# The end of a two-layer graph kernel: the last round's empty slots filled, and the last group's softmax weights transposed on TensorE without the detour through DRAM

**Chip, cores, metric.** One core of one Trainium2 chip. The metric is the device time of the core in microseconds (us), median of several runs.

## The reference, cut to what matters

128 graphs of 128 nodes with 512 features pass two layers, each with residual and layer norm:

```python
# layer 0
q, k, v = x @ Wq0.T, x @ Wk0.T, x @ Wv0.T
rel = adj.T * (q @ k.T);  rel = rel / norm(rel, axis=2)
x = layernorm(x + rel @ v)
# layer 1: 8 heads of 64
q, k, v = (x @ W + b for W, b in ((Wq,bq), (Wk,bk), (Wv,bv)))
scores = q @ k.T / 8 + where(adj == 0, -1e9, 0)
x = layernorm(x + softmax(scores) @ v)
```

All is fp32.

## The kernel before

It works on 32 groups of 4 graphs. TensorE's work is cut into slots, 35 to a round. In round r five projections run, 7 slots each: m and v0 (layer 0) of group r+1, then q, k and v1 (layer 1) of group r. All else is hung on slots as short pieces; a piece named at slot s is issued to its engines just before that slot's projection step.

The schedule of layer 1's attention, for graph b of group g:

```python
for b in range(G):
    s = 32 + 7 * b
    at(g, s, attn_scores, g, b)
    at(g, s + 1, attn_max, g, b)
    for i in range(4):
        at(g, s + 2 + i, attn_exp, g, b, 2 * i)
    at(g, s + 4, attn_spill, g, b, 0)
    at(g, s + 6, attn_spill, g, b, 1)
    at(g, s + 7, attn_stage, g, b)
    at(g, s + 12, attn_transpose, g, b)
    at(g, s + 13, attn_out, g, b)
    at(g, s + 14, attn_back, g, b)
    at(g, s + 16, attn_rows, g, b)
    at(g, s + 18, attn_sum, g, b)
    at(g, s + 20, attn_stats, g, b)
    at(g, s + 22, attn_store, g, b)
```

The kernel transposes these weights on VectorE in blocks of 32x32 (the prediction below names the page that bears on it), so the blocks of the 128x128 weights are sorted through DRAM: `attn_spill` writes them (wd), `attn_stage` reads them back in another order (wl), `attn_transpose` gives wT. The value product comes out transposed and makes a second detour (od, then the row tile o):

```python
def attn_out(g, b):
    ...
            nc.tensor.matmul(p[s*HD:(s+1)*HD, a, :], V1[g][:, b, h*HD:(h+1)*HD], wT[...])   # po
    nc.vector.transpose(oT..., p...)
    ...
def attn_rows(g, b):
    o = two.tile(..., tag="o")
    nc.sync.dma_start(o..., OD.pop((g, b))...)
    xr = two.tile([P, D], F32, tag="xr")
    nc.sync.dma_start(xr, X1D[g, b // 2][b % 2])       # residual
def attn_sum(g, b):
    nc.vector.tensor_tensor(f, f, rs..., op=ALU.mult)  # "the row product", o<-o,rs
    nc.gpsimd.tensor_tensor(xr, xr, bv_b, op=ALU.add)
    nc.gpsimd.tensor_tensor(o, o, xr..., op=ALU.add)
```

Layer 0's result also goes through DRAM, for the block order that layer 1 needs:

```python
def x1_spill(g, h):      # x1d<-x
    X1D[g, h] = dram.tile([2, P, D], F32, tag="x1d", bufs=6)
    nc.sync.dma_start(X1D[g, h]..., X[g, h])
def x1_stage(g, h):      # xl_h<-x1d, four transfers; they must wait until x1d has landed
    load_staged(g, h, X1D[g, h])
```

All these transfers are issued by one engine, SyncE, in program order.

Of the kernel before, what the change touches and what calls it, by code (L numbers as in the profile page):

```python
# [6 lines left out]

F32 = mybir.dt.float32
AF = mybir.ActivationFunctionType
ALU = mybir.AluOpType  # L10
AX = mybir.AxisListType

EPS = 1e-5
NEG = -1e9
# [3 lines left out]
def kernel(  # L18
# [15 lines left out]
    nc = tc.nc  # L34
    B, N, D = x.shape
    P = 128
    H, HD = 8, 64
    G = 4
    NG = B // G
    C = D // P  # L40
    HF = D // 2
    assert N == P and D == H * HD and B % G == 0 and G * N == D

    const = ctx.enter_context(tc.tile_pool(name="const", bufs=1))
    one = ctx.enter_context(tc.tile_pool(name="one", bufs=1))
    two = ctx.enter_context(tc.tile_pool(name="two", bufs=2))
# [64 lines left out]
    bv_b = const.tile([P, D], F32, name="bv_b")  # L111
    nc.sync.dma_start(bv_b, bass.AP(tensor=bv1.tensor, offset=bv1.offset, ap=[[0, P], [1, D]]))

    ones = const.tile([P, 1], F32, name="ones")
    nc.vector.memset(ones, 1.0)
    mhalf = const.tile([P, G], F32, name="mhalf")
    nc.vector.memset(mhalf, -0.5)

    mask = const.tile([P, D], F32, name="mask")
    for a in range(H // 2):  # L120
        nc.vector.tensor_scalar(mask.rearrange("p (q a r) -> p q a r", q=A, a=H // 2)[:, :, a, :],
# [94 lines left out]

    def x1_transpose(g, dh, h):
        if dh == 0 and h == 0:
            X1T[g] = one.tile([P, C, G, P], F32, tag="x1T", name=f"x1T_{g}")
            TX1[g] = one.tile([P, 4, 2, HF], F32, tag="tx1", name=f"tx1_{g}")  # L220
        transpose_quarter(X1T[g], g, h, dh)
        if h:
            token_sums(TX1[g], X1T[g], dh)
# [4 lines left out]
    class Projection:  # L228
# [8 lines left out]
        def begin(self):  # L237
            k, g = self.kind, self.g
            if k in ("m", "v0"):
                self.xT, self.t = XT[g], TX[g]  # L240
            else:
                self.xT, self.t = X1T[g], TX1[g]
            if k == "m":
                YT[g] = self.y = one.tile([P, C, G, P], F32, tag="yT", name=f"yT_{g}")
            elif k == "q":
                QT[g] = self.y = one.tile([P, C, G, P], F32, tag="qT", name=f"qT_{g}")
            elif k == "k":
                KT[g] = self.y = one.tile([P, C, G, P], F32, tag="kT", name=f"kT_{g}")
            elif k == "v0":
                V0[g] = self.y = one.tile([P, G, D], F32, tag="v0", name=f"v0_{g}")  # L250
            else:
                V1[g] = self.y = one.tile([P, G, D], F32, tag="v1", name=f"v1_{g}")
            self.s = one.tile([P, 3, 2, HF], F32, tag="s", name=f"s_{self.name}")

        def out(self, eh, th):
# [81 lines left out]
    def statistics(h, stats, b, tag):  # L337
        bs = small.tile([P, 6], F32, tag="bs", name=f"bs_{tag}")
        nc.vector.bn_stats(bs, h)  # L339
        nc.vector.bn_aggr(stats[:, b, :], bs)  # L340

    def inverse_std(stats, n, tag):
        ve = small.tile([P, G], F32, tag="ve", name=f"ve_{tag}")
        nc.gpsimd.tensor_scalar(ve[:, :n], stats[:, :n, 1], EPS, None, op0=ALU.add)
        rstd = small.tile([P, G], F32, tag="rstd", name=f"rstd_{tag}")
        nc.gpsimd.tensor_tensor(rstd[:, :n], ve[:, :n], mhalf[:, :n], op=ALU.pow)
        return rstd
# [28 lines left out]
    def attn_scores(g, b):  # L376

        p = ps_s.tile([P, 2, A, H // 2, Q], F32, tag="s", name=f"ps_{g}_{b}")
        for a in range(H // 2):
            for s in range(2):  # L380
                r = slice(s * HD, (s + 1) * HD)
                nc.tensor.matmul(p[:, s, :, a, :], QT[g][r, a, b, :], KT[g][r, a, b, :], start=True, stop=True)  # L382
        w = two.tile([P, 2, A, H // 2, Q], F32, tag="w", name=f"w_{g}_{b}")
        nc.vector.scalar_tensor_tensor(w.rearrange("p s q a r -> p s (q a r)"),  # L384
                                       p.rearrange("p s q a r -> p s (q a r)"), HD ** -0.5,
                                       mask[:, None, :].to_broadcast([P, 2, D]), op0=ALU.mult, op1=ALU.add)
        nmax = small.tile([P, H], F32, tag="nmax", name=f"nmax_{g}_{b}")
        sums = small.tile([P, H], F32, tag="sums", name=f"sums_{g}_{b}")
        SOFT[g, b] = [w, nmax, sums]
# [19 lines left out]

    def attn_stage(g, b):  # L410

        wl = one.tile([P, A, H, Q], F32, tag="wl", name=f"wl_{g}_{b}")
        SOFT[g, b][0] = wl
        rows = WD.pop((g, b)).rearrange("(a s) q t f -> s a q (t f)", s=Q)
        for q in range(A):
            nc.sync.dma_start(wl[q * Q:(q + 1) * Q].rearrange("p a i r -> p a (i r)"), rows[:, :, q, :])
# [61 lines left out]




    R = 35
    dense, short = {}, {}

    def at(r, k, f, *a):
        short.setdefault(R * r + k, []).append((f, a))

    for r in range(-1, NG):
        todo = [("m", r + 1), ("v0", r + 1), ("q", r), ("k", r), ("v1", r)]
        for j, (kind, g) in enumerate(todo):  # L490
            if not 0 <= g < NG:
                continue
            pr = Projection(kind, g)
            for k, i in ((0, 1), (1, 5), (3, 6), (4, 2), (5, 3), (6, 7), (9, 4)):
                dense[R * r + 7 * j + k] = (pr, i)
    halves = [(dh, h) for dh in range(2) for h in range(2)]
    for g in range(NG):

        for h in range(2):
            if g:  # L500
                at(g - 2, 12, load_staged, g, h)
                at(g - 1, 12 + 4 * h, load, g, h)
            at(g - 1, 29 + h, x1_spill, g, h)
            at(g - 1, 30 + 2 * h, x1_stage, g, h)
        for k, (dh, h) in zip((24, 25, 27, 28), halves):
            at(g - 2, k, x_transpose, g, dh, h)
        for b in range(G):
            at(g - 1, 11 + b, l0_score, g, b)
            at(g - 1, 19 + 2 * b, l0_out, g, b)
            at(g - 1, 27 + b // 2, l0_layernorm, g, b)  # L510
        at(g - 1, 16, l0_norm, g)
        at(g - 1, 26, l0_rstd, g)

        for k, (dh, h) in zip((1, 2, 4, 5) if g else (8, 9, 11, 12), halves):
            at(g, k, x1_transpose, g, dh, h)
        for b in range(G):
            s = 32 + 7 * b
            at(g, s, attn_scores, g, b)
            at(g, s + 1, attn_max, g, b)
            for i in range(4):  # L520
                at(g, s + 2 + i, attn_exp, g, b, 2 * i)
            at(g, s + 4, attn_spill, g, b, 0)
            at(g, s + 6, attn_spill, g, b, 1)
            at(g, s + 7, attn_stage, g, b)
            at(g, s + 12, attn_transpose, g, b)
            at(g, s + 13, attn_out, g, b)
            at(g, s + 14, attn_back, g, b)
            at(g, s + 16, attn_rows, g, b)
            at(g, s + 18, attn_sum, g, b)
            at(g, s + 20, attn_stats, g, b)  # L530
            at(g, s + 22, attn_store, g, b)

    with tc.manual_schedule():
        for k in range(min(short), -R):
# [41 lines left out]
```

## Time and profile before

| | before |
|---|---|
| median of 4 runs | 2,628.34 us (2,625.99 to 2,632.44) |
| span of the profiled run | 2,625.2 us |
| start of the last projection step ahead of the value product of group 29's last graph ("the anchor") | 2,484.21 us |
| from the anchor to the end ("the end part") | 141.0 us |

The prediction below shows the views that carry its reading. The anchor is added here because it is the same instruction in every kernel of this document and no change reaches its own work. One more view shows the start: after the first loads (9.88 us), this is TensorE's only long wait in the first 60 us (start, duration, engine, operation, then the idle time before it and what ended it).

```profile
43.63 3.78 PE L268 MATMUL pb_v<-wc_v,tx 128*128 128x256 f32 x8 [4.56 <-DVE yT L283]
```

VectorE is late there with yT, since masks and sums of weights stand ahead of it in its queue.

### The profile page before, as it was taken

Reading aid. Unit: us, or ns where it says so; the run is one execution under the profiler, and the core shown is the slowest. Engines: PE = TensorE matmul, PEld = TensorE weight load, DVE = VectorE, ACT = ScalarE, POOL = GpSimd, SP = SyncE. Lnnn points to the kernel's source line nnn. Section 1 sums busy time; section 2 is a strip of 40 time slices with the busy share of each in tenths; the row PEclk is TensorE's granted clock in tenths of the full one; section 3 lists DMA queues with packets and bytes.
Section 4 is the critical chain, followed back from the end, with each engine's and each line's share of the span. In section 5 each row is a group of like instructions: output and inputs, shape, how many; then the busy total and the mean of one; then the engine's idle time right before and its main releaser. Section 6 shows DMA issues by size and latency. Waiting matters only on the chain.

```text
span 2625.2 us, 41633 instructions
## 1 busy us (share of the span) xinstructions
PE 2540.0 (97%) x14624; PEld 2123.9 (81%) x14624; DVE 1607.3 (61%) x2584; ACT 1042.1 (40%) x3207; POOL 858.4 (33%) x1209
## 2 busy tenths in 40 slices
PE   7999999999999999999999999999999999999982
PEld 5788888888888888888888888888888888888861
DVE  4555665656666665666666666666666666666553
ACT  1234444444444434444344344344443434444442
POOL 4123332333332323333323333323333323333222
PEclk9999999999999999999999999999999999999985
DMA  6255556555555555555555545556545556546444
GB/s 149 68 142 167 152 167 168 155 159 165 159 159 173 158 153 168 159 155 173 164 148 176 159 149 173 161 151 176 161 146 174 161 157 174 161 142 176 152 140 130
DMA packets 518450, 412.09 MB, mean 157 GB/s; under 512 B 38240, under 2 KB 433632, under 8 KB 518240
## 3 DMA queue, kind: packets, MB, share of 16 engines
q1 hardware_dynamic: 518240, 409.43, 53.8%
q8 instruction: 115, 1.88, 0.3%
q14 instruction: 95, 0.78, 0.1%
HBM read 241.50 MB, written 167.77 MB: 156 GB/s over the span
## 4 chain that ended last, share of the span: by engine, by line
PE 93%; DMA 2%; DVE 2%; SPq 1%; POOL 1%; issue 1%; ACT 0%; DVEq 0%; POOLq 0%; ACTq 0%
PE pa_v L268 17%; PE pa_k L268 9%; PE pa_q L268 8%; PE pb_v L268 8%; PE pa_m L268 8%; PE ps L382 5%; PE po L433 5%; PE pst L320 4%; PE pd_v L268 4%; PE pb_k L268 4%; PE po L364 4%; PE pb_q L268 4%; PE pb_m L268 4%; PE pd_q L268 2%; PE pd_m L268 2%; PE pd_k L268 2%
## 5 line engine op out<-in xcount | busy, mean ns | idle before, releaser
L401 ACT ACTIVATE w<-w,nmax 128x128 f32<-128x128 f32 x1024 | 399.3, 393 | 330.4 <-DVE nmax L394 290.6
L461 POOL TENSOR_TENSOR xr<-xr,bv_b 128x512 f32<-128x512 f32 x128 | 164.1, 1282 | 694.8 <-DMA xr<-x1d 686.2
L268 PE MATMUL pa_v<-wc_v,tx 128*128 128x256 f32 x1536 | 372.2, 385 | 1.6 <-DVE v L283 1.6
L268 PEld LDWEIGHTS pa_v<-wc_v,tx 128*128 128x128 f32 x1536 | 281.7, 190 | 45.9 <-ACT kT L279 5.3
L459 DVE TENSOR_TENSOR o<-o,rs 128x512 f32<-128x512 f32 x128 | 121.8, 952 | 196.7 <-DMA o<-od 196.7
L384 DVE SCALAR_TENSOR_TENSOR w<-ps,mask 128x1024 f32<-128x1024 f32 x128 | 156.1, 1220 | 138.4 <-PE ps L382 137.8
L322 POOL TENSOR_TENSOR sq<-rel 128x128 f32<-128x128 f32 x128 | 51.6, 403 | 474.5 <-DVE rel L321 474.5
L401 ACT ACTIVATION_READ_ACCUMULATOR w<-w,nmax 128x1 f32 x1024 | 194.5, 190 | 0.0
L433 PE MATMUL po<-wT,v 128*64 128x128 f32 x2048 | 145.1, 286 | 47.5 <-DVE wT L420 46.5
L462 POOL TENSOR_TENSOR o<-o,xr 128x512 f32<-128x512 f32 x128 | 175.2, 1369 | 38.8 <-DVE o L459 27.8
L433 PEld LDWEIGHTS po<-wT,v 128*64 128x64 f32 x2048 | 113.3, 140 | 89.8 <-DVE wT L420 46.0
L268 PE MATMUL pa_q<-tx,wc_q 128*128 128x256 f32 x768 | 185.6, 385 | 0.0
L339 DVE BATCH_NORM_STATS2 bs<-o 128x6 f32<-128x512 f32 x128 | 87.8, 686 | 159.3 <-POOL o L462 159.3
L268 PE MATMUL pa_k<-tx,wc_k 128*128 128x256 f32 x768 | 184.7, 383 | 0.0
L268 PE MATMUL pa_m<-tx,wc_m 128*128 128x256 f32 x768 | 182.6, 381 | 0.3 <-ACT s_m L276 0.3
L436 DVE STREAM_TRANSPOSE oT<-po 128x512 f32<-128x512 f32 x128 | 91.8, 717 | 136.1 <-PE po L433 136.0
L268 PEld LDWEIGHTS pa_q<-tx,wc_q 128*128 128x128 f32 x768 | 144.1, 191 | 37.2 <-issue 14.6
L276 ACT COPY s_v<-pa_v 128x512 f32<-128x512 f32 x128 | 75.0, 586 | 231.6 <-PE pa_v L268 206.8
L268 PEld LDWEIGHTS pa_m<-tx,wc_m 128*128 128x128 f32 x768 | 146.8, 191 | 21.2 <-ACT s_m L276 1.0
L475 ACT ACTIVATE y<-o,sh,rstd 128x512 f32<-128x512 f32 x128 | 104.0, 813 | 149.1 <-POOL sh L354 142.5
L268 PEld LDWEIGHTS pa_k<-tx,wc_k 128*128 128x128 f32 x768 | 143.4, 190 | 23.6 <-issue 5.3
L394 DVE TENSOR_REDUCE nmax<-w 128x4 f32<-128x512 f32 x256 | 162.3, 676 | 0.1
(138 smaller groups left out, 5008.4 us busy)
## 6 DMA issues: line engine op xcount, KB each, us to landing
wd<-w SPq DMA_DIRECT2D x256, 256.0 KB, 2.5
wl<-wd SPq DMA_DIRECT2D x512, 128.0 KB, 2.8
xl_x<-in_x_dram SPq DMA_DIRECT2D x256, 128.0 KB, 5.5
x<-in_x_dram SPq DMA_DIRECT2D x64, 512.0 KB, 5.2
x1d<-x SPq DMA_DIRECT2D x64, 512.0 KB, 3.2
xl_h<-x1d SPq DMA_DIRECT2D x256, 128.0 KB, 2.6
od<-oT SPq DMA_DIRECT2D x512, 64.0 KB, 1.7
o<-od SPq DMA_DIRECT2D x128, 256.0 KB, 4.1
```

Source lines behind the costliest of these rows:

```text
L268: nc.tensor.matmul(bank[:, m, :], l[:, k, m * P:(m + 1) * P], r[:, k, :], start=start and m == 0 and k == 0, stop=(m == 1 and k == 1), ski ...
L320: nc.tensor.matmul(p, XT[g][:, dc, b, :], YT[g][:, dc, b, :], start=(dc == 0), stop=(dc == C - 1))
L364: nc.tensor.matmul(p, REL[g][0][:, b, :], V0[g][:, b, :], start=True, stop=True)
L382: nc.tensor.matmul(p[:, s, :, a, :], QT[g][r, a, b, :], KT[g][r, a, b, :], start=True, stop=True)
L384: nc.vector.scalar_tensor_tensor(w.rearrange("p s q a r -> p s (q a r)"), p.rearrange("p s q a r -> p s (q a r)"), HD ** -0.5, mask[:, Non ...
L394: nc.vector.tensor_reduce(nmax[:, s * (H // 2):(s + 1) * (H // 2)], w[:, s].rearrange("p q a r -> p a q r"), axis=AX.XY, op=ALU.max, negat ...
L401: nc.scalar.activation(w[:, s, :, a, :], w[:, s, :, a, :], AF.Exp, bias=nmax[:, i:i + 1], accum_out=sums[:, i:i + 1])
L433: nc.tensor.matmul(p[s * HD:(s + 1) * HD, a, :], V1[g][:, b, h * HD:(h + 1) * HD], wT[:, s * (H // 2) + a].rearrange("p q t -> p (q t)"), ...
L459: nc.vector.tensor_tensor(f, f, rs.rearrange("p s y a -> p (s y a)")[:, :, None].to_broadcast([P, A * H // 2, Q]), op=ALU.mult)
L461: nc.gpsimd.tensor_tensor(xr, xr, bv_b, op=ALU.add)
L462: nc.gpsimd.tensor_tensor(o, o, xr.rearrange("p (a f r) -> p f a r", a=H // 2, f=A), op=ALU.add)
L475: nc.scalar.activation(y.rearrange("p (a f r) -> p f a r", a=H // 2, f=A), o, AF.Identity, bias=sh[:, 0:1], scale=rstd[:, 0:1])
```

## The change

Intent: (1) In the last round there is no group 32, so m and v0 leave 14 empty slots; q, k and v1 of the last group move up into them, its layer 0 finishes a few slots earlier, and the attention of group 30 follows in 3 slots a graph, not 7. (2) The last group's weights stay on the chip: scores in plain head order, transposes on TensorE against an identity, a value product that comes out in rows, no wd, wl, od, o.

Cut to its core (lines with tags of buffers left out):

```diff
+    ident = const.tile([P, P], F32, name="ident")
+    make_identity(nc, ident)
+    maskp = const.tile([P, N], F32, name="maskp")
+    nc.vector.tensor_scalar(maskp, adj_sb, 0.0, NEG, op0=ALU.is_equal, op1=ALU.mult)
...
+    def last_residual(g):
+        LT["x"] = one.tile([P, G, D], F32, tag="qT", name=f"xr_{g}")
+        for h in range(2):
+            xr = LT["x"][:, 2 * h:2 * h + 2, :]
+            nc.sync.dma_start(xr, X1D[g, h].rearrange("b n d -> n b d"))
+            nc.gpsimd.tensor_tensor(xr, xr, bv_b[:, None, :].to_broadcast([P, 2, D]), op=ALU.add)
...
+    def last_transpose(g, b, s):
...
+        p = ps_m.tile([P, H // 2, P], F32, tag="m", name=f"pwT_{g}_{b}_{s}")
+        for a in range(H // 2):
+            nc.tensor.transpose(p[:, a, :], SOFT[g, b][0][:, s * (H // 2) + a, :], ident)
+        nc.vector.tensor_copy(LT[b // 2][:, b % 2, s * (H // 2):(s + 1) * (H // 2), :], p)
+
+    def last_out(g, b):
...
+        p = ps_b.tile([P, H, HD], F32, tag="d", name=f"po1_{g}_{b}")
+        for h in range(H):
+            nc.tensor.matmul(p[:, h, :], LT[b // 2][:, b % 2, h % 2 * (H // 2) + h // 2, :],
+                             V1[g][:, b, h * HD:(h + 1) * HD], start=True, stop=True)
...
+        nc.vector.tensor_tensor(o..., p, rs..., op=ALU.mult)
+        nc.vector.tensor_tensor(o, o, xr, op=ALU.add)
+        ... statistics, last_store: scale and store
...
-        todo = [("m", r + 1), ("v0", r + 1), ("q", r), ("k", r), ("v1", r)]
+        todo = [("m", r + 1), ("v0", r + 1)] if r < NG - 1 else []
+        todo += [("q", r), ("k", r), ("v1", r)]
...
-            at(g - 1, 29 + h, x1_spill, g, h)
-            at(g - 1, 30 + 2 * h, x1_stage, g, h)
+            at(g - 1, (25 if last else 29) + h, x1_spill, g, h)
+            at(g - 1, (26 if last else 30) + 2 * h, x1_stage, g, h)
...
+        if last:
+            at(g, 11, last_residual, g)
         for b in range(G):
-            s = 32 + 7 * b
+            if last:
+                at(g, (17, 18, 20, 21)[b], last_scores, g, b)
+                for i in range(2):
+                    at(g, 19 + 2 * b + i, last_exp, g, b, i)
+                    at(g, 21 + 2 * b + i, last_transpose, g, b, i)
+                at(g, 24 + 2 * b, last_out, g, b)
+                at(g, 26 + 2 * b, last_store, g, b)
+                continue
+            s = 32 + (3 if g == NG - 2 else 7) * b
...
+            pieces = attn_transpose, attn_out, attn_back, attn_rows, attn_sum, attn_stats, attn_store
+            for k, f in zip((11, 12, 13, 15, 16, 19, 22) if g == NG - 2 else (12, 13, 14, 16, 18, 20, 22), pieces):
+                at(g, s + k, f, g, b)
```

More of the change, by code (lines that the diff above doesn't have):

```diff
@@ L5 @@
 from concourse import mybir
+from concourse.masks import make_identity
 from concourse._compat import with_exitstack
@@ L218, in x1_transpose @@
         if dh == 0 and h == 0:
-            X1T[g] = one.tile([P, C, G, P], F32, tag="x1T", name=f"x1T_{g}")
-            TX1[g] = one.tile([P, 4, 2, HF], F32, tag="tx1", name=f"tx1_{g}")
+            X1T[g] = one.tile([P, C, G, P], F32, tag="x1T" if g < NG - 1 else "xT", name=f"x1T_{g}")
+            TX1[g] = one.tile([P, 4, 2, HF], F32, tag="tx1" if g < NG - 1 else "tx", name=f"tx1_{g}")
         transpose_quarter(X1T[g], g, h, dh)
@@ L245, in begin @@
             elif k == "q":
-                QT[g] = self.y = one.tile([P, C, G, P], F32, tag="qT", name=f"qT_{g}")
+                QT[g] = self.y = one.tile([P, C, G, P], F32, tag="qT" if g < NG - 1 else "yT", name=f"qT_{g}")
             elif k == "k":
@@ L251, in begin @@
             else:
-                V1[g] = self.y = one.tile([P, G, D], F32, tag="v1", name=f"v1_{g}")
+                V1[g] = self.y = one.tile([P, G, D], F32, tag="v1" if g < NG - 1 else "v0", name=f"v1_{g}")
             self.s = one.tile([P, 3, 2, HF], F32, tag="s", name=f"s_{self.name}")
@@ L382, in attn_scores @@
                 nc.tensor.matmul(p[:, s, :, a, :], QT[g][r, a, b, :], KT[g][r, a, b, :], start=True, stop=True)
-        w = two.tile([P, 2, A, H // 2, Q], F32, tag="w", name=f"w_{g}_{b}")
+        w = two.tile([P, 2, A, H // 2, Q], F32, tag="xl" if g == NG - 2 and b >= 2 else "w", name=f"w_{g}_{b}")
         nc.vector.scalar_tensor_tensor(w.rearrange("p s q a r -> p s (q a r)"),
@@ L410, in attn_stage @@
     def attn_stage(g, b):
-        wl = one.tile([P, A, H, Q], F32, tag="wl", name=f"wl_{g}_{b}")
+        wl = one.tile([P, A, H, Q], F32, tag=("wl", "tx1", "wl", "x1T")[b] if g == NG - 2 else "wl", name=f"wl_{g}_{b}")
         SOFT[g, b][0] = wl
@@ L477, in attn_store, with last_scores @@
         nc.sync.dma_start(out[g * G + b], y)
+    LT = {}
+    def last_residual(g):
[4 more added lines that the diff above has]
+            nc.gpsimd.tensor_tensor(xr, xr, bv_b[:, None, :].to_broadcast([P, 2, D]), op=ALU.add)
+    def last_scores(g, b):
+        p = ps_s.tile([P, 2, H // 2, P], F32, tag="s", name=f"ps_{g}_{b}")
+        for a in range(H // 2):
+            for s in range(2):
+                r = slice(s * HD, (s + 1) * HD)
+                nc.tensor.matmul(p[:, s, a, :], QT[g][r, a, b, :], KT[g][r, a, b, :], start=True, stop=True)
+        w = two.tile([P, H, P], F32, tag="w" if b < 2 else "xl", name=f"w_{g}_{b}")
+        nc.vector.scalar_tensor_tensor(w, p.rearrange("p s a j -> p (s a) j"), HD ** -0.5,
+                                       maskp[:, None, :].to_broadcast([P, H, P]), op0=ALU.mult, op1=ALU.add)
+        nmax = small.tile([P, H], F32, tag="nmax", name=f"nmax_{g}_{b}")
+        nc.vector.tensor_reduce(nmax, w, axis=AX.X, op=ALU.max, negate=True)
+        sums = small.tile([P, H], F32, tag="sums", name=f"sums_{g}_{b}")
+        SOFT[g, b] = w, nmax, sums, LT["x"][:, b, :]
@@ new lines, in last_exp @@
+    def last_exp(g, b, s):
+        w, nmax, sums, _ = SOFT[g, b]
+        for i in range(s * (H // 2), (s + 1) * (H // 2)):
+            nc.scalar.activation(w[:, i, :], w[:, i, :], AF.Exp, bias=nmax[:, i:i + 1], accum_out=sums[:, i:i + 1])
+    def last_transpose(g, b, s):
+        if b % 2 == 0 and s == 0:
+            LT[b // 2] = one.tile([P, 2, H, P], F32, tag="tx1" if b else "x1T", name=f"wT_{g}_{b}")
+        p = ps_m.tile([P, H // 2, P], F32, tag="m", name=f"pwT_{g}_{b}_{s}")
+        for a in range(H // 2):
+            nc.tensor.transpose(p[:, a, :], SOFT[g, b][0][:, s * (H // 2) + a, :], ident)
+        nc.vector.tensor_copy(LT[b // 2][:, b % 2, s * (H // 2):(s + 1) * (H // 2), :], p)
@@ new lines, in last_out @@
+    def last_out(g, b):
+        _, _, sums, xr = SOFT.pop((g, b))
+        rs = small.tile([P, H], F32, tag="rs", name=f"rs_{g}_{b}")
+        nc.vector.reciprocal(rs.rearrange("p (a s) -> p s a", s=2), sums.rearrange("p (s a) -> p s a", s=2))
+        p = ps_b.tile([P, H, HD], F32, tag="d", name=f"po1_{g}_{b}")
+        for h in range(H):
+            nc.tensor.matmul(p[:, h, :], LT[b // 2][:, b % 2, h % 2 * (H // 2) + h // 2, :],
+                             V1[g][:, b, h * HD:(h + 1) * HD], start=True, stop=True)
+        if b == 0:
+            LT["o"] = one.tile([P, G, D], F32, tag="v1", name=f"o_{g}")
+        o = LT["o"][:, b, :]
+        nc.vector.tensor_tensor(o.rearrange("p (h e) -> p h e", h=H), p,
+                                rs[:, :, None].to_broadcast([P, H, HD]), op=ALU.mult)
+        nc.vector.tensor_tensor(o, o, xr, op=ALU.add)
+        stats = small.tile([P, 1, 2], F32, tag="stats1", name=f"st1_{g}_{b}")
+        statistics(o, stats, 0, f"1_{g}_{b}")
+        SOFT[g, b] = o, stats, inverse_std(stats, 1, f"1_{g}_{b}")
@@ L482, with last_store @@
+    def last_store(g, b):
+        o, stats, rstd = SOFT.pop((g, b))
+        nc.vector.tensor_scalar(o, o, stats[:, 0, 0:1], rstd[:, 0:1], op0=ALU.subtract, op1=ALU.mult)
+        nc.sync.dma_start(out[g * G + b], o)
     R = 35
@@ L502 @@
                 at(g - 1, 12 + 4 * h, load, g, h)
-            at(g - 1, 29 + h, x1_spill, g, h)
-            at(g - 1, 30 + 2 * h, x1_stage, g, h)
+        last = g == NG - 1
+        for h in range(2):
+            at(g - 1, (25 if last else 29) + h, x1_spill, g, h)
+            at(g - 1, (26 if last else 30) + 2 * h, x1_stage, g, h)
         for k, (dh, h) in zip((24, 25, 27, 28), halves):
@@ L508 @@
             at(g - 1, 11 + b, l0_score, g, b)
-            at(g - 1, 19 + 2 * b, l0_out, g, b)
-            at(g - 1, 27 + b // 2, l0_layernorm, g, b)
+            at(g - 1, (18, 19, 21, 22)[b] if last else 19 + 2 * b, l0_out, g, b)
+            at(g - 1, (24 if last else 27) + b // 2, l0_layernorm, g, b)
         at(g - 1, 16, l0_norm, g)
-        at(g - 1, 26, l0_rstd, g)
-        for k, (dh, h) in zip((1, 2, 4, 5) if g else (8, 9, 11, 12), halves):
+        at(g - 1, 23 if last else 26, l0_rstd, g)
+        for k, (dh, h) in zip((8, 9, 11, 12) if g == 0 else (-4, -3, -2, -1) if last else (1, 2, 4, 5), halves):
             at(g, k, x1_transpose, g, dh, h)
+        if last:
+            at(g, 11, last_residual, g)
         for b in range(G):
-            s = 32 + 7 * b
+            if last:
[7 more added lines that the diff above has]
+            s = 32 + (3 if g == NG - 2 else 7) * b
             at(g, s, attn_scores, g, b)
@@ L524 @@
             at(g, s + 7, attn_stage, g, b)
-            at(g, s + 12, attn_transpose, g, b)
-            at(g, s + 13, attn_out, g, b)
-            at(g, s + 14, attn_back, g, b)
-            at(g, s + 16, attn_rows, g, b)
-            at(g, s + 18, attn_sum, g, b)
-            at(g, s + 20, attn_stats, g, b)
-            at(g, s + 22, attn_store, g, b)
+            pieces = attn_transpose, attn_out, attn_back, attn_rows, attn_sum, attn_stats, attn_store
+            for k, f in zip((11, 12, 13, 15, 16, 19, 22) if g == NG - 2 else (12, 13, 14, 16, 18, 20, 22), pieces):
+                at(g, s + k, f, g, b)
     with tc.manual_schedule():
```

## The prediction

> **What bounds the kernel now.** I first read the page's busy shares and its 40 slices:
>
> ```profile
> PE 2540.0 (97%) x14624; PEld 2123.9 (81%) x14624; DVE 1607.3 (61%) x2584; ACT 1042.1 (40%) x3207; POOL 858.4 (33%) x1209
> ...
> PE   7999999999999999999999999999999999999982
> ...
> PEclk9999999999999999999999999999999999999985
> ```
>
> TensorE is full from the second slice to the 38th, so up to about 2,495 us nothing but its instruction count matters, and the change leaves that count alone. Only the last two slices can be shortened. So I asked for the busy times of three stretches: the last full round, what follows until the last projection ends, and the rest.
>
> ```profile
> 2417.10:2498.20 81.10, 80.31 (x465) 66.95 (x463) 46.77 (x78) 33.88 (x108) 23.98 (x36) 1.00 0.50 155
> 2498.20:2560.90 62.70, 50.62 (x299) 42.05 (x298) 33.97 (x50) 24.42 (x88) 19.42 (x28) 0.89 0.45 135
> 2560.90:2625.20 64.30, 12.72 (x113) 10.61 (x112) 22.65 (x35) 14.11 (x54) 17.41 (x29) 0.58 0.43 129
> ```
>
> Columns: length, then busy time of TensorE, weight load, VectorE (DVE), ScalarE (ACT), GpSimd (POOL), granted clock, DMA share, GB/s. The last projections have 12.1 us of holes and a clock of 0.89; the last 64.3 us have a fifth of TensorE, and no engine is busy for more than 22.7 us: a chain of latencies. The timeline of TensorE shows both:
>
> ```profile
> 2498.23 1.16 PE L382 MATMUL ps<-kT,qT 64*128 64x128 f32 x16
> 2506.99 1.98 PE L433 MATMUL po<-wT,v 128*64 128x128 f32 x16 [7.60 <-DVE wT L420]
> ...
> 2519.15 1.74 PE L433 MATMUL po<-wT,v 128*64 128x128 f32 x16 [3.70 <-DVE wT L420]
> ...
> 2560.88 1.16 PE L382 MATMUL ps<-kT,qT 64*128 64x128 f32 x16
> 2567.49 1.98 PE L433 MATMUL po<-wT,v 128*64 128x128 f32 x16 [5.45 <-DVE wT L420]
> ...
> 2579.27 1.98 PE L433 MATMUL po<-wT,v 128*64 128x128 f32 x16 [8.14 <-DVE wT L420]
> ...
> 2593.52 1.97 PE L433 MATMUL po<-wT,v 128*64 128x128 f32 x16 [10.26 <-DVE wT L420]
> 2606.82 1.97 PE L433 MATMUL po<-wT,v 128*64 128x128 f32 x16 [11.33 <-DVE wT L420]
> ```
>
> The holes at 2,507 and 2,519 us are the empty slots of the last round (no projections m and v0 of a 33rd group). The four last rows are the last group's four graphs, 11.8, 14.2 and 13.3 us apart, the end 18.4 us after the last. What a graph waits for is in the waits from 2,488 us on (total, times, longest):
>
> ```profile
> POOL xr L461 <- DMA xr<-x1d: 80.8, 9, 13.4
> PE po L433 <- DVE wT L420: 46.5, 6, 11.3
> ...
> DVE o L459 <- DMA o<-od: 28.8, 7, 8.1
> ```
>
> The named releaser wT had itself stood in DVE's queue behind the product `o` (L459) of the graph before, and that behind its trip through DRAM (od, then o). So each graph costs its two detours in series.
>
> **What the Trainium skill says.** "VectorE: DVE Perf Modes", The three transpose paths: VectorE transposes only 32x32 blocks, TensorE a full 128x128 into PSUM. That is why the kernel sorts blocks through DRAM, and the trace agrees: wd 2.5 us and wl 2.8 us to landing around a transpose of 1.24 us. "TensorE: Matmul & The Clock Gate", What's actually happening: about 3.4 us of idleness halve the clock. The trace agrees: 16 `po` matmuls take 1.09 us in the full rounds and 1.97 after the holes above. The same page, Part 4: PE-mode transpose, says transposes need a copy out of PSUM and do not count as busy for that gate; no transpose runs before, so this is untested. Its part Architectural detail says ScalarE and VectorE are strict FIFO, which the wT wait just told agrees with.
>
> **The change part by part.** I compared the instruction order of both kernels on each engine: the same up to the middle of the round before the last, except at the start.
>
> *Start.* The identity is built on an idle GpSimd. One mask more on VectorE: four like it take 3.23 us (L121), so 0.8 us, while TensorE at 43.6 us waits for VectorE. +0.8 us.
>
> *Last group's layer 0, earlier.* Its last `po` (L364) moves from 2,474.9 to about 2,468.5 us. From there to normalized rows it took 6.1 us before, so they stand at 2,474.6; spill and staging follow in the sync queue (3.2 and 2.7 us a landing, 1.8 us to issue four): second half staged near 2,491.3. Of the four block transposes that q needs, the first stands ready before its first product at 2,496.6, the second before its next one at 2,498.5; the others have 6 us more. I count no stall.
>
> *Dense part.* From the scores of graph 0 of group 30, at 2,489.0 us in both, TensorE has before its last projection step: 25 steps at 1.75 us (1.73, or 1.92 after another kind) 43.8; 8 scores at 1.09 8.7; 4 `po` at 1.02 4.1; three sets of transposes, 8 passes like `pst` (0.89 us), 2.7. Sum 59.3. Stalls, by walking the queues with measured durations: wT of group 30's third graph stands behind a row load that lands at 2,526.5, 1.7 us; scores of the last group wait for ScalarE to empty kT, 0.9 us. End near 2,551.7, against 2,560.9.
>
> *Tail.* Here the last group no longer goes to DRAM. ScalarE is not the limit: exps follow each other in 0.385 us, 3.1 a graph, done by 2,558. VectorE is: for each graph two PSUM copies (0.6 each, by the 0.59 of similar ones from start to start), reciprocal 0.15, product out of PSUM 0.7, residual 0.6, statistics 0.8, last scaling 0.45: 3.9 us, times four 15.6. One copy is done before, one statistic of group 30 (0.8) comes in: 15.8 from 2,552.7. Waits of VectorE for `po` (16 passes at 0.1 like `pn`, 1.6, less what lies between) and for GpSimd's rstd: 1.0+0.2+0.8+0.6+1.0 = 3.6. Last store, as before from 2,622.2 to 2,625.2: 3.0. Together 2,575.1. Where the clock falls, `po` and transposes double on that path: three graphs at 1.2, 3.6 us. So 2,578.7, with the start 2,579.5. Runs lie 3.4 above the span (2,628.6 to 2,625.2): about **2,582 us**, 1.8% less.
>
> Of the 46 us, 9 come from the filled slots, 37 from the tail (64.3 to about 27).
>
> **Rivals.** *(1) The sync queue and DMA become the bound of the last round.* Group 30's graphs follow each other in 3 slots, not 7. A graph's issues cost 2.06 (wd) + 1.80 (wl) + 1.77 (od) + 0.37 + 0.34 + 0.45 = 6.8 us, and 3 slots are 3 x 2.2 = 6.6; its 2 MB ask for 300 GB/s where the page's best slice has 176. For: any wait in that queue shifts all behind it. Against: 2 to 5 us of slack at two of the four `po` in my walk. It would stall each later `po`, in order on TensorE: span 2,585 to 2,600. *(2) VectorE's queue.* Statistics of group 30 wait for GpSimd, which first adds the bias to the last group's 1 MB residual (128x1024 twice, 2.5 us each at 1.27 per 512), and the last group's projections and masks stand behind them. I already have VectorE waiting to 2,533.3 there; it lies beside a TensorE wait, but residual rows landing 2 us late give 2 us: 2,577 to 2,585. *(3) All smooth.* Transposes in one pass, clock kept, scaling at twice the rate: 8 us less, 2,571, over 2% faster. *(4) Layer 0's staging late*: DVE's FIFO then holds the mask of graph 1; some 2 us.
>
> **Range and chances.** Two rivals add, one takes off, and the walk has little room below 2,571: 2,571 to 2,600. The line for 2% is 2,576.1, 6 below my number, less than one spread (about 9): faster 0.27, within 2% 0.71, slower 0.02.
>
> **What would show it.** Right if: up to 2,489 us both traces agree to 1 us; q of the last group follows with no hole over 1 us; the last projection ends at 2,549 to 2,555; the last 25 us have VectorE over 70% busy and no detour; the granted clock falls there. Wrong if TensorE in the last round waits several times over 2 us for wT (rival 1), or if statistics of group 30 hold VectorE over 3 us (rival 2), or if the tail after the last projection is under 20 us (rival 3).

## The result, and the profile after

| | before | after |
|---|---|---|
| median of 4 runs | 2,628.34 us | 2,599.12 us (2,597.51 to 2,599.69) |
| ratio | | 0.9886, 95% interval 0.9869 to 0.9903 |
| span of the profiled run | 2,625.2 us | 2,597.9 us |
| anchor | 2,484.21 us | 2,488.74 us |
| end part | 141.0 us | 109.2 us |

The kernel is 29 us faster, where 46 were predicted: inside the range, but only 0.9 us from its upper end of 2,600. In the end part 32 us were gained; 4.5 us went before it.

Busy shares and slices of the kernel after:

```profile
PE 2545.7 (98%) x14656; PEld 2129.9 (82%) x14656; DVE 1610.4 (62%) x2589; ACT 1037.6 (40%) x3203; POOL 851.7 (33%) x1197
...
PE   7999999999999999999999999999999999999996
...
PEclk9999999999999999999999999999999999999997
```

TensorE is now full up to the last slice. The stretches of the end (length, busy time of TensorE, weight load, VectorE, ScalarE, GpSimd, granted clock, DMA share, GB/s), cut at the first scores of group 30, the first scores of the last group, and the end of the last projection:

```profile
2421.50:2500.00 78.50, 73.60 (x417) 61.40 (x415) 41.62 (x70) 29.25 (x90) 23.19 (x35) 0.98 0.48 144
2500.00:2552.20 52.20, 45.68 (x273) 38.00 (x272) 31.22 (x43) 21.76 (x84) 17.56 (x18) 0.93 0.53 160
2552.20:2568.80 16.60, 16.52 (x134) 13.66 (x134) 14.16 (x18) 10.75 (x45) 5.24 (x7) 1.00 0.36 113
2568.80:2597.90 29.10, 15.63 (x85) 14.32 (x83) 18.32 (x37) 6.84 (x27) 8.51 (x18) 0.65 0.14 55
```

The tail shrank from 64.3 to 29.1 us, close to the 27 predicted. But TensorE idles 4.9 us in the first stretch, where it idled 0.8 before, and 6.5 us in the second. Its timeline shows the two holes and the tail:

```profile
2495.53 1.97 PE L440 MATMUL po<-wT,v 128*64 128x128 f32 x16 [4.90 <-DVE wT L427]
...
2545.29 1.97 PE L440 MATMUL po<-wT,v 128*64 128x128 f32 x16 [6.52 <-DVE wT L427]
2547.19 3.37 PE L274 MATMUL pb_v<-wc_v,tx 128*128 128x256 f32 x8
...
2570.91 1.77 PE L530 MATMUL po<-v,wT 128*128 128x64 f32 x14 [1.78 <-DVE wT L522]
...
2576.25 2.31 PE L530 MATMUL po<-v,wT 128*128 128x64 f32 x14 [2.34 <-DVE wT L522]
...
2581.59 3.25 PE L530 MATMUL po<-v,wT 128*128 128x64 f32 x14 [1.00 <-DVE wT L522]
...
2587.87 3.25 PE L530 MATMUL po<-v,wT 128*128 128x64 f32 x14 [1.55 <-DVE wT L522]
```

Call them **hole A** (2,490.6 to 2,495.5 us, value product of group 29's last graph) and **hole B** (2,538.8 to 2,545.3 us, third graph of group 30). Each is followed by slow work: 1.97 us for 16 matmuls that take 1.09 us at full clock, 3.37 us for a projection step of 1.89.

The waits from 2,488 us on (total, times, longest) name the releaser, and what the releaser itself had waited for:

```profile
DVE o L466 <- DMA o<-od: 12.6, 2, 7.4
...
PE po L440 <- DVE wT L427: 11.4, 2, 6.5
```

The same chain as in the holes of the kernel before: wT stands in VectorE's queue behind a row product that waits for its rows o. Why the rows are late differs. For hole A, SyncE's issues:

```profile
2483.62 0.38 SPq L217 DMA_DIRECT2D x1d<-x  x1
...
2487.23 1.79 SPq L89 DMA_DIRECT2D xl_h<-x1d  x4
...
2489.62 0.41 SPq L457 DMA_DIRECT2D o<-od  x1
```

In the kernel before, the same row load went out ahead of the spill, so none stood behind the wait for the landing of x1d:

```profile
2478.81 0.34 SPq L450 DMA_DIRECT2D o<-od  x1
...
2481.12 0.37 SPq L212 DMA_DIRECT2D x1d<-x  x1
2484.21 1.80 SPq L88 DMA_DIRECT2D xl_h<-x1d  x4
```

The staging xl_h may not be issued before x1d has landed, so in the changed kernel SyncE stood still from 2,484.5 to 2,487.2 us; then came four issues of 1.79 us and another spill, and only then the row load, which landed at 2,493.6. The change moved spill and staging of the last group four slots up, in front of this load. For hole B, first SyncE, then VectorE, then GpSimd:

```profile
2532.88 1.13 SPq L494 DMA_DIRECT2D xr<-x1d  x2
2534.10 0.47 SPq L457 DMA_DIRECT2D o<-od  x1
```
```profile
2541.25 2.14 DVE L466 TENSOR_TENSOR o<-o,rs 128x512 f32<-128x512 f32 x1 [5.14 <-DMA o<-od]
```
```profile
2538.20 4.63 POOL L495 TENSOR_TENSOR xr<-xr,bv_b 128x1024 f32<-128x1024 f32 x2 [22.22 <-DMA xr<-x1d]
```

The row load of 256 KB was issued right behind the residual's 1 MB and landed after 7.1 us (the page's median for such a load is 4.1). Then the row product took 2.14 us in place of 0.69, while GpSimd added the bias to that residual.

At the start the wait of 4.56 us before the change became 7.11:

```profile
46.16 3.78 PE L274 MATMUL pb_v<-wc_v,tx 128*128 128x256 f32 x8 [7.11 <-DVE yT L289]
```

### The profile page after: what moved, and what is told of

The parts are those of the page before. It is cut to its first block, busy times and chain, and to the rows that moved or that the text cites. A ratio compares the mean times of both kernels' runs of the same rounds, so it can differ in the third digit from the quotient of the medians.

```text
span 2597.9 us, 41593 instructions
## 1 busy us (share of the span) xinstructions
PE 2545.7 (98%) x14656; PEld 2129.9 (82%) x14656; DVE 1610.4 (62%) x2589; ACT 1037.6 (40%) x3203; POOL 851.7 (33%) x1197
## 4 chain that ended last, share of the span: by engine, by line
PE 92%; DMA 3%; DVE 2%; SPq 1%; issue 1%; POOL 0%; ACT 0%; DVEq 0%; POOLq 0%; ACTq 0%
PE pa_v L274 16%; PE pa_q L274 9%; PE pb_v L274 8%; PE pa_k L274 8%; PE pa_m L274 8%; PE ps L388 5%; PE po L440 5%; PE pst L326 4%; PE pd_v L274 4%; PE pb_q L274 4%; PE po L370 4%; PE pb_k L274 4%; PE pb_m L274 4%; PE pd_q L274 2%; PE pd_m L274 2%; PE pd_k L274 2%
## 5 line engine op out<-in xcount | busy, mean ns | idle before, releaser
L408 ACT ACTIVATE w<-w,nmax 128x128 f32<-128x128 f32 x992 | 386.8, 393 | 313.3 <-DVE nmax L401 296.8
L408 ACT ACTIVATION_READ_ACCUMULATOR w<-w,nmax 128x1 f32 x992 | 188.4, 190 | 0.0
L469 POOL TENSOR_TENSOR o<-o,xr 128x512 f32<-128x512 f32 x124 | 169.2, 1364 | 35.3 <-DVE o L466 24.2
L388 PEld LDWEIGHTS ps<-kT,qT 64*128 64x128 f32 x1984 | 120.4, 187 | 41.1 <-issue 40.8
L427 DVE STREAM_TRANSPOSE wT<-wl 128x1024 f32<-128x1024 f32 x124 | 153.1, 1235 | 0.0
L440 PEld LDWEIGHTS po<-wT,v 128*64 128x64 f32 x1984 | 107.2, 138 | 54.9 <-issue 26.5
```

What stands on the lines that cost most here:

```text
L388: nc.tensor.matmul(p[:, s, :, a, :], QT[g][r, a, b, :], KT[g][r, a, b, :], start=True, stop=True)
L408: nc.scalar.activation(w[:, s, :, a, :], w[:, s, :, a, :], AF.Exp, bias=nmax[:, i:i + 1], accum_out=sums[:, i:i + 1])
L427: nc.vector.transpose(wT, SOFT[g, b][0].rearrange("p a i r -> p i a r"))
L440: nc.tensor.matmul(p[s * HD:(s + 1) * HD, a, :], V1[g][:, b, h * HD:(h + 1) * HD], wT[:, s * (H // 2) + a].rearrange("p q t -> p (q t)"), ...
L469: nc.gpsimd.tensor_tensor(o, o, xr.rearrange("p (a f r) -> p f a r", a=H // 2, f=A), op=ALU.add)
```

## The experiments

They ran in three batches of four, each batch on one chip beside the kernel before. "End part" is the span of the profiled run from the anchor on. One profile of one kernel leaves about 3 us of doubt in it: the changed kernel run again (last experiment) had 112.6 in place of 109.2 us, with slower clock in the same places.

| kernel | median us | ratio to before | end part us | hole A / B us |
|---|---|---|---|---|
| before | 2,633 to 2,634 on these chips | 1 | 141.0 | none there |
| after, first / again | 2,599.12 / 2,600.67 | 0.9886 / 0.9881 | 109.2 / 112.6 | 4.90 / 6.52, 5.36 / 6.19 |
| e1_rows_first | 2,595.13 | 0.9858 | 102.1 | 0.20 / 5.63 |
| e2_residual_late | 2,600.99 | 0.9875 | 108.0 | 5.35 / 1.62 |
| e3_mask_late | 2,600.54 | 0.9876 | 111.4 | 5.20 / 5.66 |
| e4_all_three | 2,593.42 | 0.9848 | 102.3 | 0.42 / 1.83 |
| e5_resident | 2,587.27 | 0.9819 | 97.8 | 0.40 / 1.79 |
| e6_out_later | 2,582.61 | 0.9808 | 93.0 | 0.40 / 1.86 |
| e7_slots_only | 2,621.10 | 0.9954 | 130.2 | 5.70 / 2.15 |
| e8_transposes_only | 2,607.46 | 0.9899 | 114.1 | none / other place |
| e9_keep_busy | 2,581.05 | 0.9802 | 92.4 | none / 1.59 |
| e10_best | 2,579.34 | 0.9793 | 89.8 | 0.34 / 0.30 |
| e11_transposes_resident | 2,600.46 | 0.9877 | 110.7 | none / none |

The 95% intervals reach some 0.0015 to each side of the ratio; 0.001 is 2.6 us. All gave correct results.

**Theory:** the two holes come from the order of SyncE's queue (spill and staging before a row load; 1 MB before a row load), not from its throughput. **Rivals:** the queue or the DMA engines are simply full there; or VectorE's and GpSimd's own work is what holds wT back.

### Row load ahead of the staging

```diff
+                if g == NG - 3 and b == 2 and f is attn_rows:
+                    k -= 1
```

> The changed kernel, but the row loads (o, xr) of group 29's third graph are issued one slot earlier, ahead of the staging of the last group's layer-0 result. No transfer is added or removed. Theory A (the sync queue's order: the row load stood behind an issue that waited 3.1 us for the spill x1d to land, so VectorE's product o and behind it wT came late): the hole of 4.9 us at 2,495.5 us shrinks to under 2 us, the clock stays up, and the time falls by 4 to 7 us, to 2,592-2,595. Rival B (the DMA engines are simply full there): the hole stays above 4 us and the time within 1.5 us of 2,599.

Measured: ratio 0.9858, interval 0.9842 to 0.9875; some 6 to 7 us less than the changed kernel (the two intervals just overlap; the profile decides). Hole A is gone:

```profile
2491.87 1.09 PE L440 MATMUL po<-wT,v 128*64 128x128 f32 x16 [0.20 <-DVE wT L427]
```

The same transfers, with the loads of one graph (o and xr) one slot earlier, and 4.7 us of wait and the slow clock after it vanish. So hole A was order, not throughput. Hole B stays, as it should.

### Residual loaded late

```diff
-            at(g, 11, last_residual, g)
+            at(g, 18, last_residual, g)     # the two loads
+            at(g, 22, last_bias, g)         # the bias additions on GpSimd
```

> The changed kernel, but the last group's residual rows (two loads of 512 KB) are issued at slot 18 in place of 11, behind the row loads of group 30's first three graphs, and their bias is added at slot 22. Theory A (the 1 MB ahead of graph 0's row load o makes it land 7.1 us after its issue, and VectorE, in order, keeps kT and wT of graph 2 behind it): the hole of 6.5 us at 2,545 us shrinks to under 2.5 us, o lands within 4 us, and the time falls by 5 to 8 us, to 2,591-2,594. Rival B (the spacing of 3 slots is too tight for the sync queue whatever is loaded): the hole stays above 4 us, the time falls by less than 2 us.

Measured: hole B shrank from 6.52 to 1.62 us, but the ratio, 0.9875 (0.986 to 0.989), does not differ from that of the changed kernel. VectorE and TensorE show where the gain went:

```profile
2575.11 2.81 DVE L542 TENSOR_TENSOR o<-o,xr 128x512 f32<-128x512 f32 x1 [2.95 <-POOL xr L499]
```
```profile
2579.49 3.25 PE L535 MATMUL po<-v,wT 128*128 128x64 f32 x14 [6.03 <-DVE wT L526]
```

GpSimd came to the bias additions only at 2,572.73 us, directly after group 30's additions that stood ahead of them, so the residual was late in the tail instead. Hole B's cause lies in the residual's load and addition, and they cannot be moved into the tail for free. This run moves both. Two others part them: in e1_rows_first and e3_mask_late the row load stands behind the same 1 MB and lands 7.4 us after its issue, but the row product is hardly slowed (0.94 and 0.85 us), and the hole is still 5.63 and 5.66 us. So most of hole B is the load. In e1_rows_first:

```profile
2536.37 0.94 DVE L466 TENSOR_TENSOR o<-o,rs 128x512 f32<-128x512 f32 x1 [5.45 <-DMA o<-od]
```

### Fifth mask built later

```diff
-    nc.vector.tensor_scalar(maskp, adj_sb, ...)      # at the start
+    at(2, 20, plain_mask)                            # the same instruction, in round 2
```

> The changed kernel, but the added mask (one VectorE instruction of 0.66 us) is built in round 2 instead of the start. Theory A (in the start VectorE is on the path and contends with GpSimd, so 0.66 us of work cost 2.5 us): the wait of TensorE at 46 us goes back from 7.1 to 4.6 us, the time falls by 2 to 3 us, to about 2,596.5. Rival B (only its own length counts): it falls by 0.7 us or less.

Measured: the first wait is 4.56 us again, exactly as before the change, and pb_v starts at 44.09 us, 2.1 us earlier than in the changed kernel. The time, ratio 0.9876 (0.9862 to 0.9891), cannot be told from that of the changed kernel: its profile lost 2.2 us again in the end part, where the same work ran at a slower clock. The wait is settled, its worth in the total is not.

### All three together

> The three edits together. If the three causes are separate, their gains add: 2.5 + 6.5 + 6.5, so about 2,583 us (2,580 to 2,588). If the first two are one backlog of the same queue, the sum is smaller: 2,588 to 2,592. My prediction's walk with these holes left out would give 2,582.

Measured: 0.9848 (0.9834 to 0.9863), about 9 us less than the changed kernel, and outside both ranges that were expected. It is hardly better than the first edit alone, since the late residual sends two waits of 3.5 us into the tail.

### Residual not loaded at all

The residual of the last group is still in its tile X on the chip, since no later group overwrites it. With the first and third edits:

```diff
-            nc.sync.dma_start(xr, X1D[g, h].rearrange("b n d -> n b d"))
-            nc.gpsimd.tensor_tensor(xr, xr, bv_b..., op=ALU.add)
+            nc.gpsimd.tensor_tensor(X[g, h], X[g, h], bv_b..., op=ALU.add)
-        SOFT[g, b] = w, nmax, sums, LT["x"][:, b, :]
+        SOFT[g, b] = w, nmax, sums, graph(g, b)
-            at(g, 11, last_residual, g)
+            at(g, 6, last_residual, g)
```

> Rows first and mask late as in the runs before, and the last group's residual is not loaded at all: it is read from the tile of layer-0 rows, which nothing overwrites after the last group; GpSimd adds the bias there at slot 6. 1 MB of loads goes. Theory A (the 1 MB only moved its delay: with it late, the load o of group 30's last graph came late, and with it the first copy of the tail): the hole at wT of graph 2 stays under 2 us, the first two `po` of the tail no longer wait 3.5 us each, ratio to the kernel before 0.979 to 0.983, 4 to 7 us under the run with all three edits (0.9848). Rival B (the tail alternates between TensorE at half clock and VectorE whatever is loaded): the ratio stays at 0.984 or above.

Measured: 0.9819 (0.9802 to 0.9835), 6 to 8 us less than with the late load, as expected, and no new wait in the tail. Hole B is down to 1.79 us. In what is left the rows of a graph are still waited for 1.85 us, though their load now lands 4.8 us after its issue.

### The output of each graph later, on two banks

Over the kernel just told, `last_out` one slot later, and its PSUM bank alternating:

```diff
-        p = ps_b.tile([P, H, HD], F32, tag="d", name=f"po1_{g}_{b}")
+        p = ps_b.tile([P, H, HD], F32, tag="b" if b % 2 else "d", name=f"po1_{g}_{b}")
-                at(g, 24 + 2 * b, last_out, g, b)
-                at(g, 26 + 2 * b, last_store, g, b)
+                at(g, 25 + 2 * b, last_out, g, b)
+                at(g, 27 + 2 * b, last_store, g, b)
```

> The same, and each graph's product `po` of the last group is issued one slot later, behind both transposes of the next graph, with two PSUM banks in turn; so VectorE copies the next graph's weights before it starts this one's product and statistics. Theory A (the tail's step is a closed loop: 14 `po` passes 3.25 us at half clock, 0.73 product, 0.72 residual, 0.9 statistics, 0.6 copy = 6.2 us a graph): the step falls to 4 to 4.5 us, the last four graphs take 5 to 6 us less, ratio about 0.978. Rival B (exps or GpSimd set the step): under 2 us less.

Measured: 0.9808 (0.9794 to 0.9823), where about 0.978 was expected; the interval overlaps with that of e5_resident, but the end part is 4.8 us shorter. The slot and the bank were changed together, so this run does not say what each is worth. In the changed kernel and in e5_resident one graph of the tail takes up to 6.3 us, in a ring: product 3.25 us at the slow clock, then on VectorE scaling out of PSUM 0.73, residual 0.72, statistics 0.9 and the copy of the next weights 0.6, then the next product. With the copies ahead of the product, VectorE no longer waits for the product and a graph takes 4.2 us. Two starts of the scaling out of PSUM show it:

```profile
2565.50 0.69 DVE L531 TENSOR_TENSOR o<-po,rs 128x512 f32<-128x512 f32 x1
...
2569.70 0.69 DVE L531 TENSOR_TENSOR o<-po,rs 128x512 f32<-128x512 f32 x1
```

### The two halves of the change apart

Slots only: the last group keeps its detours, 3 slots a graph from slot 17.

> One half of the change alone: the early layer 0, the filled slots and group 30 at 3 slots, but the last group keeps the detour through DRAM, at 3 slots from slot 17. My prediction put 9 us of its 46 on the slots: about 0.996 (2,617 to 2,622 us for 2,628). Rival (the delays measured in the round before the last eat it): 0.998 to 1.001.

Transposes only: slots as before, the pieces of the last group 14 slots later, the residual loaded at slot 25.

> The other half alone: the slots of the kernel before, with the two empty ones, group 30 at 7 slots, but the last group's weights transposed on TensorE. My prediction put 37 us on the tail: about 0.986. If the delays that the changed kernel shows come from the tighter slots, this run has no hole before wT of group 29 and none behind the residual; it would then be as fast as the whole change (0.9886), which would say that the slots brought nothing.

Measured: slots 0.9954 (0.9939 to 0.9969), transposes 0.9899 (0.9885 to 0.9914). Against before, that is 12 and 27 us, where 9 and 37 were predicted. Their sum, 39 us, exceeds the 30 to 31 us of both together: on top of the transposes the slots bring only 4 us. So the two together fall some 8 us short of the sum, and with intervals of 4 us on each ratio that is only just clear of noise. The holes do not account for it, for each part alone has its own: 5.70 and 2.15 us with the slots, 4.48 with the transposes, 11.4 with both. The profiles place it in the tail. Alone, the slots shorten the stretch after the last projection from 64.3 to about 55.5 us; on top of the transposes they don't (26.7 us without them, 29.1 with). Both parts shorten the same chain; no run tests this further. The slots create hole A by themselves (5.70 us). With the transposes only, a hole of 4.48 us appears behind the residual's load too, with the same signs as hole B:

```profile
2557.52 2.64 DVE L466 TENSOR_TENSOR o<-o,rs 128x512 f32<-128x512 f32 x1 [5.08 <-DMA o<-od]
```

### Transposes only, residual not loaded

The second half with the edit of e5_resident (no load, bias in place on GpSimd at slot 14):

> The kernel e8_transposes_only (the transposes without the change's slots) with the residual read from the tile that is on the chip, so that no 1 MB load stands in the sync queue. If the 4.48 us hole there comes from the o load that lies behind the residual, it goes, and the kernel is 5 to 7 us faster than e8_transposes_only: ratio about 0.987. Then the slots of the change add little once the queue is free. Rival: the hole comes from the VectorE addition beside GpSimd; then it stays above 3 us and the ratio is 0.989 to 0.990.

Measured: 0.9877 (0.9862 to 0.9891), 5.8 us less, and the hole is gone (no wait at that product). This run moves the bias addition too (to slot 14), so it does not part the load from the addition; the two row products do: here the wait for the row load is 1.13 us, where it was 5.08, and the product takes 0.69 us, where it took 2.64. So 4.0 us went with the load and 2.0 with the slow work beside GpSimd. The rival has the smaller share. The text also said that the slots would then add little. That was wrong. The end part is 110.7 us here and 97.8 in e5_resident, which differs in it by the slots and the earlier row load: freed of hole A, the slots are worth about 13 us. Alone, with hole A in them, they took 10.8 us from the end part.

### Spare matmuls that keep the clock up

e5_resident with four spare 128x256 matmuls, results never read, ahead of each `last_out`:

```diff
+    def keep_busy(n, name):
+        junk = ps_a.tile([P, 2, HF], F32, tag="a", name=f"junk_{name}")
+        for i in range(n):
+            nc.tensor.matmul(junk[:, i % 2, :], wc["q"][:, 0, 0, 0:P], wc["k"][:, 0, 0, :], start=True, stop=True)
...
     def last_out(g, b):
+        keep_busy(4, b)
```

> The kernel e5_resident with four spare 128x256 matmuls (results never read) on a free PSUM bank ahead of the output's transposes of each graph. The question is whether the half clock is part of the 6.28 us that one graph of the tail takes. If ordinary matmuls keep the clock up where transposes do not, the 14 passes of the product take 1.77 us in place of 3.25 us, the step goes from 6.28 to about 4.8 us, and the kernel is 3 to 5 us faster than e5_resident (ratio about 0.980). Rival: the step is set by VectorE's queue and not by the clock, or the spare work stands in the path itself; then the time is that of e5_resident or longer (ratio 0.982 to 0.984).

Measured: ratio 0.9802 (0.9788 to 0.9817); the intervals overlap with that of e5_resident, but the end part is 5.4 us shorter and the mechanism shows. The tail of e5_resident, then that of this kernel:

```profile
2557.00:2587.70 30.70, 18.45 (x85) 17.23 (x83) 17.69 (x36) 6.84 (x27) 8.53 (x18) 0.54 0.14 52
```
```profile
2552.10:2578.10 26.00, 17.10 (x117) 15.57 (x116) 18.37 (x37) 6.84 (x27) 8.52 (x18) 0.89 0.16 61
```

With 32 matmul instructions more, TensorE is busy for a shorter time: the clock is 0.89 in place of 0.54, the product takes 1.77 us in place of 3.25, and each of the last graphs 4.8 to 5.0 us in place of 6.3. Whether the clock stayed up because ordinary matmuls count and transposes don't, or because the gaps got shorter (at most 0.8 us between products, where they were 1.0 to 1.8), this run doesn't tell.

### The best version

e6_out_later with group 30's row products two slots later, after the wT of the graph two further on:

```diff
-            for k, f in zip((11, 12, 13, 15, 16, 19, 22) if g == NG - 2 else ...
+            for k, f in zip((11, 12, 13, 15, 18, 20, 22) if g == NG - 2 else ...
```

(The text below calls these "the last projection's row products"; meant are those of group 30, which run during the last projections.)

> The kernel e6_out_later with the last projection's row products one slot pattern later (each after the value product of the graph two further on, the statistics a slot after). If the rest of the second hole (1.8 us) and the first product's wait for the row bias in the tail (1.8 us) come only from the order of these pieces, it is about 3 us faster than e6_out_later: ratio 0.979 to 0.980. Rival: the waits move to the next piece in the queue, and the ratio stays at 0.981.

Measured: 2,579.34 us, ratio 0.9793 (0.9777 to 0.981), as expected; the interval overlaps with that of e6_out_later (0.9808, in another batch). In the same batch the kernel before took 2,633.22 and the changed kernel 2,600.67 us (0.9881, interval 0.9865 to 0.9898), so it beats both. What is left of hole B is 0.30 us:

```profile
2532.91 1.09 PE L439 MATMUL po<-wT,v 128*64 128x128 f32 x16 [0.30 <-DVE wT L426]
```

### The control

> The changed kernel again, unaltered, as the control on this chip: ratio 0.988 to 0.989, with both holes ahead of the value products of groups 29 and 31 (4.9 and 6.5 us of wait).

Measured: 0.9881, both holes there (5.36 and 6.19 us). As expected. (The second hole is ahead of a value product of group 30, not 31 as the text says.)

## Why the prediction was right, and where it erred

The class (within 2%) and the range held, the number was 17 us too low. (To get from span to time the prediction added 3.4 us, the median before less the span of the profiled run. That run itself took 2,626.94 us, 1.7 above its span; after the change it is 1.8.) By its own steps, on the profiled spans (2,597.9 against 2,579.5, so 18.4 us):

| step | predicted us | measured us | difference |
|---|---|---|---|
| start: one mask | 0.8 | 2.3 (2.5 at the first pb_v, 2.9 from 64 us, 2.3 from 82 us on) | +1.5 |
| middle: "the same" | 0 | 2.2, what is left of 4.5 at the anchor | +2.2 |
| staging: "I count no stall" | 0 | 6.5 (wait 4.90, slow work after it 1.6) | +6.5 |
| dense part, scores of group 30 to the last projection | 61.9 | 68.8 (2,500.0 to 2,568.8) | +6.9 |
| tail | 27.0 | 29.1 | +2.1 |
| the prediction's own sum | | | −0.8 |

The last row: 2,489.0 + 61.9 is 2,550.9, not 2,551.7; the start's 0.8 us seems to be in twice.

*Start.* The mask took 0.66 us, where 0.8 was estimated. But it pushed the additions for wc_v so that they met GpSimd's additions rather than its copies: two took 1.64 and 1.63 us, where they had 0.96 and 0.98, and the other masks 3.87 in place of 3.23. That is 0.6 + 0.64 + 0.68 + 0.65 = 2.6. The Trainium skill bears on the additions, "SBUF — State Buffer", SBUF: two separate sides: a VectorE operation with two inputs in SBUF and a GpSimd operation that reads SBUF lock each other out. The trace fits as far as the lengths go: where additions of both overlap, VectorE's take 1.63 to 1.74 us and GpSimd's 1.59 to 1.70, where 1.27 is their shortest. Why the masks, with one input, grew too is not shown. e3_mask_late gave the old wait back.

*Middle.* "Up to 2,489 us both traces agree to 1 us" failed: the anchor is 4.5 us later. Beyond the start, the rest is scattered: TensorE's waits between 100 and 2,488 us come to 2.7 us, where they were 1.0 before, none over 1.0. Waits differ from run to run; the profiled run of the control reached the anchor another 4.1 us later. Their cause was not looked for.

*Staging: the step that failed.* The prediction followed the staged rows to the one who uses them, q of the last group. That was right: q follows without a hole. It did not ask who stands behind the staging in SyncE's queue. It was the row load of group 29, and through VectorE's queue the value product. e1_rows_first shows it: one load one slot earlier, 4.7 us of wait gone.

*Dense part: the second step that failed, by the same omission.* A stall of 1.7 us at the third graph of group 30 was in the sum, "behind a row load". The wait was 6.52 us, and the slow clock after it cost 2.3 more; all the rest came to 0.2 less than planned (the three sets of transposes took 1.7 us in place of 2.7, at half the passes: rival 3 had that right). So the last projection ended at 2,568.8 us, not at 2,549 to 2,555. The prediction had the residual in view, but only as GpSimd's work and VectorE's wait (rival 2), not as 1 MB ahead of the row load in the queue. The Trainium skill says that descriptors are taken in ring order on each DMA engine ("DMA: Bandwidth & Descriptors", Queues, rings and completion order). That a small load behind a large one lands late is what one would infer from it; the 7.1 us here fit, and so do the runs without the load: the wait at this place is 1.8 us in e5_resident and none in e11_transposes_resident. In e7_slots_only, with the same 3 slots and no such load, it is 2.15 us.

*Tail: mechanism half right.* The detours are gone and the clock falls, as said. But "VectorE over 70% busy" came to 63% (18.32 of 29.1 us): it was not VectorE's sum of 3.9 us a graph that set the pace but a ring of TensorE and VectorE of up to 6.3 us. That the total came out near was luck in part. e6_out_later opened the ring, and VectorE alone then sets 4.2 us, near the 3.9.

*Rivals.* Rival 1 named the place, SyncE's queue, and the size (2,585 to 2,600). Its mechanism, throughput, did not hold: between 2,500.0 and 2,552.2 us the DMA moved 160 GB/s, less than the 176 of the best slice before. Rival 2's slow VectorE work showed in the row product of 2.14 us. Rival 1 also said that each later value product would stall; of group 30's four one did. What came was an order problem, which the prediction had listed under rival 1 as "any wait in that queue shifts all behind it" and then weighed away by slack at the products, not at the loads.

*Where the missing gain went.* Most of it is the two holes with the slow clock after them: 6.5 us of hole A, and 7.1 of hole B beyond the planned 1.7. e10_best, without them and with the ring open, is 54 us faster than before (2,633.22 to 2,579.34). By parts, 9 us were predicted for the slots and 37 for the tail; alone they gave 12 and 27, and why they do not add up is told above as far as it is known.

## What to carry to other kernels

When a transfer is moved up in an in-order queue, follow not only the one who uses its data but every load that now stands behind it, and what waits for that load: an issue that must wait for an earlier landing holds up every load behind it (2.7 us here). Before loading a residual again, look whether its tile is still on the chip. In a tail of small steps, look for rings between two engines; issuing the next step's copies before this step's product opens them.

## What the Trainium skill lacked or had wrong

- "TensorE: Matmul & The Clock Gate", HAM oscillation: the rule under this heading is about idle gaps above some 3.4 us (elsewhere the page speaks of short idle times too, without a length). In the tail of e5_resident no gap between TensorE's instructions before its last product was over 1.8 us, and yet each product from 2,565 us on ran at 3.25 us in place of 1.77. The page gives no share of busy time below which the clock falls; 18.45 busy of 30.7 us did not hold it (0.54), 17.10 of 26.0 with spare matmuls did (0.89). Nor does that share order the runs: e10_best kept 0.79 with 13.04 of 25.5.
- The same page, Part 4: PE-mode transpose, gives 390 ns alone and about 275 ns in a kernel for one 128x128 transpose in bf16. Here, in fp32, one is listed with 0.27 us at full clock, as there, and with 0.42 in the slow stretches. What the page lacks is the spacing: of four in a row, the next instruction started 0.53 us after the first, 0.13 us each.
- "DMA: Bandwidth & Descriptors", Queues, rings and completion order, gives the ring order but no time for a small load behind a large one: 7.1 us for 256 KB behind 1 MB here, 4.1 in the median. No page that was read shows what SyncE's wait for a landing costs the loads behind it: 2.7 us of standing still, and a row load issued at 2,489.62 us.
- "SBUF — State Buffer", SBUF: two separate sides, fits: a row product took 2.14 to 2.64 us beside GpSimd's additions, 0.69 alone. The page gives no such figure for fp32 products.
